# The conv's two values from the preceding half in the second state-space layer: two small VectorE operations in place of three ScalarE activations

## The chip, the cores and the metric

The kernel runs on one core of one Trainium2 chip. The metric is the device time of one execution in microseconds (us). A core has a matrix engine (TensorE, PE in the profile), a vector engine (VectorE, DVE), an activation engine (ScalarE, ACT), a general engine (GpSimd, POOL) and a queue engine that issues transfers (SyncE, SP). They run side by side, each works off its own queue in order, and they wait for each other by semaphores. SBUF is the on-chip memory of 128 partitions; PSUM is the smaller memory that TensorE writes to.

## The reference, cut to what matters

The network has four residual layers over x of shape [8, 384, 32, 32]: a state-space layer (L0), a deformable convolution (L1), a second state-space layer with a layer norm and a small MLP (L2), and a depthwise convolution with shifts (L3). The change touches L2. Its beginning, for each of the 8 samples with 1024 tokens:

```python
t = (t - mu) * jax.lax.rsqrt(var + 1e-05) * ln_w + ln_b
xz = t @ in_proj_w.T
xm, z = jnp.split(xz, 2, axis=-1)
K = conv_w.shape[-1]                      # 3
xp = jnp.pad(xm, ((0, 0), (K - 1, 0), (0, 0)))
xc = sum((xp[:, k:k + L, :] * conv_w[:, k] for k in range(K))) + conv_b
xc = jax.nn.silu(xc)
...
def step(hst, inp):
    dA_t, dBu_t, C_t = inp
    hst = dA_t * hst + dBu_t
    return (hst, jnp.einsum('bdn,bn->bd', hst, C_t))
```

Here `xm` has 768 channels. The conv runs over time, each channel by itself: a token's value is made of its own input (weight 2), the one before it (weight 1) and the one before that (weight 0). So when the 1024 tokens are worked on in two halves, the first two tokens of the second half need the last two inputs of the first half.

## The kernel before, in words

Both state-space layers are built by one function, `ssm_layer`. The change is in its inner functions `conv_last` and `conv`. A sample's 1024 tokens are cut into two halves of TS = 512 (`s["h"]` is 0 or 1), so a layer has 16 steps, one for each half. The 768 channels are cut into ND = 6 blocks of 128 partitions.

A step has 48 units: 6 channel blocks times 8 units. For each unit i, the main loop gives out the same work:

- ScalarE writes the decays `da` of unit i+2 (line 531, two instructions, into one of two PSUM tiles).
- VectorE runs the recurrence over time (`scan`, line 551, reads `da` in PSUM and `db` in SBUF).
- The states are multiplied by C: by VectorE for 5 units of 8 (line 564, `hs <- da, bc`, `da` in PSUM), by GpSimd for units 0, 2 and 5 of each block (line 562, both in SBUF; in those units the scan writes `hs` itself).
- GpSimd makes the inputs `db` of unit i+3 (line 539, `dub` times `bc`, both in SBUF). `db` has three buffers, so the `db` of unit i+3 takes the place of that of unit i, and can begin when scan i has ended.
- In the first half of a sample, ScalarE copies the last states of a unit (`keep_last`, line 557). In units 0, 2 and 5 GpSimd's line 562 overwrites `hs` in place, and so waits for that copy.
- TensorE sums over the states (line 574).

Around these, four lists written out by hand (`act`, `dve`, `pool`, `pe`, built by `plan`) say at which unit other work is put: the gate and the close of this half, the output projection and MLP of the half before, and the norm, input projection, conv and steps of the *next* half. The order of each engine's queue is as written (a manual schedule): in a unit ScalarE first takes its list, then the state copy and the decays; VectorE takes scan, product, then its list; GpSimd `db`, the product in its units, then its list.

The input projection of block d of the next half (`inner`, line 364) is put at unit 16, 17, 18, 24, 25 or 26 on TensorE. It takes one of three PSUM tiles that all projections share. One unit later ScalarE runs `conv_last`: line 389 writes bias plus the weight-2 product from PSUM to `u` in SBUF. Then:

- If the half in work is a first half, ScalarE saves the last two inputs to `halo` (line 391), a small SBUF tile of two columns for each block, for the second half of that sample.
- If it is a second half, ScalarE adds the three products of `halo` to the first two columns of `u` (line 397, three activations of one column each, `u <- halo * weight + u`).

Another unit later VectorE runs `conv` (line 405): two instructions that add the weight-1 and the weight-0 product from PSUM to `u`, over 511 and 510 columns. Behind them in VectorE's queue is the next unit's scan. In units 18 and 26 the close of a block (lines 593 and 594) stands ahead of the conv, in units 20 and 28 line 464.

The layer L0 uses `conv_last` and `conv` for its very first half alone, which is a first half; its other convs run on TensorE. So line 397 runs in L2 only: 8 second halves times 6 blocks times 3, 144 times.

Of the kernel before, what the change touches and what calls it, by code (L numbers as in the profile page):

```python
# [9 lines left out]
AF = mybir.ActivationFunctionType  # L10
ALU = mybir.AluOpType
# [73 lines left out]
V_CW, V_CB, V_DB, V_D, V_A = 0, 18, 24, 30, 36  # L85
# [17 lines left out]
class Net:  # L103
# [112 lines left out]
    def ssm_layer(self, li, src, dst, shift=None):  # L216
        tc, nc, ins = self.tc, self.nc, self.ins
# [4 lines left out]
        with ExitStack() as ctx:  # L222
# [49 lines left out]
            def v(i):  # L272
                return vec[:, i : i + 1]
# [113 lines left out]
            def conv_last(s, d):  # L387
                ps, ud = s["in", d], s["u"][:, d, :]
                nc.scalar.activation(ud, ps, AF.Identity, bias=v(V_CB + d), scale=v(V_CW + 3 * d + 2))
                if s["h"] == 0:  # L390
                    nc.scalar.copy(s["sib"]["halo"][:, d, :], ps[:, TS - 2 : TS])
                else:

                    halo = s["halo"][:, d, :]
                    for i, k, wi in ((0, 0, 0), (0, 1, 1), (1, 1, 0)):
                        c = ud[:, i : i + 1]
                        nc.scalar.activation(
                            c, halo[:, k : k + 1], AF.Identity, bias=c, scale=v(V_CW + 3 * d + wi)
                        )

            def conv(s, d):
                ps, ud = s["in", d], s["u"][:, d, :]
                w0, w1 = v(V_CW + 3 * d), v(V_CW + 3 * d + 1)
                for i, wi in ((1, w1), (2, w0)):
                    nc.vector.scalar_tensor_tensor(
                        ud[:, i:], ps[:, : TS - i], wi, ud[:, i:], ALU.mult, ALU.add
                    )
# [285 lines left out]
            def plan(prev, s, nxt):  # L693
# [54 lines left out]
                for d, t in enumerate(TI):  # L748
                    put(pe, t - 2, fetch_in, nxt, d)
                    put(pe, t, inner, nxt, d)  # L750
                    if mlp:
                        put(act, t + 1, conv_last, nxt, d)
                        put(dve, t + 2, conv, nxt, d)
                    else:
                        put(act, t + 1, conv_in, nxt, d)
                        put(pe, TCV[d], conv_pe, nxt, d)
                        put(act, TCO[d], conv_out, nxt, d)
# [35 lines left out]
            with tc.manual_schedule(engines=ENGINES):  # L793
                s = steps[0]
# [12 lines left out]
                for d in range(ND):  # L807
                    fetch_in(s, d)
                    inner(s, d)
                    conv_last(s, d)  # L810
                    conv(s, d)
                    if d == ND - 2:
                        silu(s, 0, ND // 2)
# [20 lines left out]
                for i, (s, j, m) in enumerate(units):  # L834
                    c, t = divmod(i, T)
# [1322 lines left out]
```

## Time and profile before

| what | value |
|---|---|
| median of 3 runs | 8728.45 us (8723.46 to 8728.67) |
| profiled execution, its own time | 8722.48 us |
| its span in the profile | 8720.7 us |
| granted TensorE clock, mean | 0.912 |
| GpSimd line 539, `db` | 1536 times, 2357 ns each |
| GpSimd line 562, `hs` | 576 times, 2356 ns each |
| VectorE line 551, scan into `da` | 960 times, 2285 ns each |
| VectorE line 564, product | 960 times, 1225 ns each |
| VectorE line 405, conv | 102 times 743 and 102 times 749 ns |
| ScalarE line 389, conv's first product | 102 times, median 777 ns |
| ScalarE line 391, saving `halo` | 54 times, median 149 ns |

The span is the stretch from the first to the last instruction that the profiler recorded. The profile has several views. The page gives busy times for the whole span; the groups give one line for each source line, engine and shape, with count, total busy time and mean duration (after the bar: total us, mean ns, then the idle time of the engine just before). The timeline gives instructions in order: start in us, duration in us, engine, line, operation, what is written and read, shape, and, in brackets, how long the engine sat idle before and what ended that. "x2" merges neighbours. The chain of waits is the path that ended last, followed back from the last instruction by the semaphores' times.

### The profile page before, as it was taken

Reading aid. Unit: us, or ns where it says so; the run is one execution under the profiler, and the core shown is the slowest. Engines: PE = TensorE matmul, PEld = TensorE weight load, DVE = VectorE, ACT = ScalarE, POOL = GpSimd, SP = SyncE. Lnnn points to the kernel's source line nnn. Section 1 sums busy time; section 2 is a strip of 40 time slices with the busy share of each in tenths; the row PEclk is TensorE's granted clock in tenths of the full one; section 3 lists DMA queues with packets and bytes.
Section 4 is the critical chain, followed back from the end, with each engine's and each line's share of the span. In section 5 each row is a group of like instructions: output and inputs, shape, how many; then the busy total and the mean of one; then the engine's idle time right before and its main releaser. Section 6 shows DMA issues by size and latency. Waiting matters only on the chain. (4 is left out here: it accounts for less than half of the span.)

```text
span 8720.7 us, 91254 instructions
## 1 busy us (share of the span) xinstructions
PE 7387.2 (85%) x29688; PEld 3825.2 (44%) x29688; DVE 7519.7 (86%) x8480; ACT 5832.6 (67%) x9518; POOL 5569.8 (64%) x3383
## 2 busy tenths in 40 slices
PE   7888888888886899999999985788888888888878
PEld 2232233223222788888787871233333333333323
DVE  6999999999997788988988895888988989888884
ACT  6777777777774556666666665676767777776761
POOL 6999999999998000000000005998998989898984
PEclk8899899889987999999999997898998899999989
DMA  4555555555553754565456434565666666565657
GB/s 126 126 126 123 120 124 125 118 122 125 125 126 99 186 133 110 130 166 127 103 148 159 122 76 122 131 153 144 156 156 156 149 147 153 141 157 142 154 152 152
DMA packets 796928, 1179.29 MB, mean 135 GB/s; under 512 B 260402, under 2 KB 413010, under 8 KB 762648
## 3 DMA queue, kind: packets, MB, share of 16 engines
q1 hardware_dynamic: 739444, 1157.23, 54.0%
q10 hardware_dynamic: 55540, 10.05, 0.7%
q0 software_dynamic: 1456, 6.07, 0.2%
q8 instruction: 237, 3.88, 0.2%
q14 instruction: 251, 2.06, 0.1%
HBM read 984.15 MB, written 188.98 MB: 135 GB/s over the span
## 5 line engine op out<-in xcount | busy, mean ns | idle before, releaser
L539 POOL TENSOR_TENSOR db<-dub,bc 128x1024 f32<-128x1024 f32 x1536 | 3606.2, 2357 | 369.1 <-DVE hs L551 169.1
L531 ACT ACTIVATE da<-dtb,vec 128x512 f32<-128x512 f32 x3072 | 2122.2, 691 | 610.5 <-DVE hs L564 407.9
L551 DVE TENSOR_TENSOR_SCAN da<-da,db 128x1024 f32<-128x1024 f32 x960 | 2193.2, 2285 | 130.5 <-ACT da L531 86.1
L472 POOL TENSOR_TENSOR dt<-dt,sp_e 128x512 f32<-128x512 f32 x96 | 122.3, 1274 | 2468.0 <-DMA bc<-bcd 2463.7
L1803 PE MATMUL wacc<-fsm,fxk 128*128 128x195 f32 (+21 forms) x10624 | 1574.9, 306 | 98.6 <-DVE fsm L1766 69.4
L1803 PEld LDWEIGHTS wacc<-fsm,fxk 128*128 128x128 f32 x10624 | 1481.2, 195 | 232.8 <-DVE fsm L1766 140.5
L551 DVE TENSOR_TENSOR_SCAN hs<-da,db 128x1024 f32<-128x1024 f32 x576 | 1315.3, 2283 | 195.6 <-POOL db L524 84.0
L562 POOL TENSOR_TENSOR hs<-hs,bc 128x1024 f32<-128x1024 f32 x576 | 1357.0, 2356 | 34.1 <-ACT st L557 34.1
L564 DVE TENSOR_TENSOR hs<-da,bc 128x1024 f32<-128x1024 f32 x960 | 1175.6, 1225 | 122.4 <-PE y L574 72.9
L574 PE MATMUL y<-hs,cols 128*32 128x512 f32 x6144 | 968.6, 649 | 282.5 <-POOL hs L562 260.1
L1766 DVE TENSOR_TENSOR fsm<-fhy,fhx 128x585 f32<-128x585 f32 (+39 forms) x3136 | 1011.2, 389 | 85.8 <-PE wacc L1803 77.0
L1749 DVE TENSOR_TENSOR fxk<-fxt,fwk 128x1024 f32<-128x1024 f32 (+1 forms) x688 | 813.4, 1182 | 9.7 <-DMA fxt<-fxd 8.7
L1726 ACT ACTIVATE fhy<-fpyx,cell 128x416 f32<-128x416 f32 (+10 forms) x832 | 422.4, 580 | 315.2 <-DVE fsm L1766 315.2
L574 PEld LDWEIGHTS y<-hs,cols 128*32 128x32 f32 x6144 | 189.1, 113 | 1002.4 <-issue 507.7
L651 PE MATMUL ps_m<-hid,wm 128*128 128x512 f32 x1152 | 549.9, 632 | 61.9 <-ACT hid L646 27.8
L632 PE MATMUL ps_h<-t,wm 128*128 128x512 f32 x1152 | 533.4, 607 | 56.5 <-DVE sp_e L464 24.2
L1709 ACT ACTIVATE fhx<-fpyx,cell 128x352 f32<-128x352 f32 (+9 forms) x640 | 344.5, 610 | 294.6 <-DVE fsm L1766 264.1
L364 PE MATMUL ps_in<-xn,winr 128*128 128x512 f32 x576 | 326.4, 713 | 176.6 <-ACT xn L353 127.0
L651 PEld LDWEIGHTS ps_m<-hid,wm 128*128 128x128 f32 x1152 | 226.8, 203 | 395.1 <-issue 283.5
L632 PEld LDWEIGHTS ps_h<-t,wm 128*128 128x128 f32 x1152 | 217.0, 194 | 376.6 <-issue 275.6
L583 PE MATMUL ps_z<-xn,winr 128*128 128x512 f32 x576 | 301.5, 672 | 47.7 <-DVE sp_e L464 47.7
L606 PE MATMUL ps_o<-u,wm 128*128 128x512 f32 x576 | 279.9, 636 | 41.5 <-DMA wm<-in_wout 36.3
(239 smaller groups left out, 9885.4 us busy)
## 6 DMA issues: line engine op xcount, KB each, us to landing
dtb<-dtd SPq DMA_DIRECT2D x768, 256.0 KB
dub<-dtd SPq DMA_DIRECT2D x768, 256.0 KB
fpyx<-fposd SPq DMA_DIRECT2D x104, 1024.0 KB
fxt<-fxd SPq DMA_DIRECT2D x96, 1024.0 KB
wm<-in_w SPq DMA_DIRECT2D x96, 768.0 KB
bc<-bcd SPq DMA_DIRECT2D x256, 256.0 KB
x<-x SPq DMA_DIRECT2D x73, 768.0 KB
dtd<-dt SPq DMA_DIRECT2D x192, 256.0 KB
```

The costliest lines, as they stand in the source:

```text
L531: nc.scalar.activation(da[:, i, :], s["dtb", j][:, k, :], AF.Exp, scale=na[:, j, n + i : n + i + 1])
L539: nc.gpsimd.tensor_tensor(db, du, s["bc"][p][:, 0], ALU.mult)
L551: nc.vector.tensor_tensor_scan(h1, da1, db1, 0.0, ALU.mult, ALU.add)
L562: nc.gpsimd.tensor_tensor(s["hs", m], s["hs", m], c, ALU.mult)
L564: nc.vector.tensor_tensor(hs_tile(s, m), s["da", m], c, ALU.mult)
L574: nc.tensor.matmul(s["y"][k * IP : (k + 1) * IP, :], sel, s["hs", p * NSUB + k][:, i, :], start=mlp and p == 0 and i == 0, stop=p == NQP - ...
L632: nc.tensor.matmul(ps, s["w1", q][:, k, f * P : (f + 1) * P], s["t"][:, k, :], start=(k == 0), stop=(k == G - 1))
L651: nc.tensor.matmul(ps, s["w2", q][:, f, o * P : (o + 1) * P], s["hid", q][:, f, :], start=(f == 0), stop=(f == 3))
L1726: nc.scalar.activation(hy[:, at : at + (yb - ya) * W], s["pyx", j][:, 0, ya * W : yb * W], AF.Abs, bias=bias)
L1749: nc.vector.tensor_tensor(t[:, :n], x, wk[:, j : j + 1, :].to_broadcast([P, n, P]), ALU.mult)
L1766: nc.vector.tensor_tensor(self.sub(sm, at, [(r * w, n), (w, r), (1, w)]), self.sub(hy, hy_at[by] + xa, [(r * W, n), (W, r), (1, w)]), self ...
L1803: nc.tensor.matmul(a[:, ya - 4 * o : yb - 4 * o, xa:xb], k, self.sub(sm, sm_at[by], [(w, yb - ya), (1, w)]), start=o not in s["open"], sto ...
```

## The change

For a second half, `conv_last` no longer adds the `halo` products on ScalarE. `conv` adds them on VectorE, ahead of its two large instructions: one `scalar_tensor_tensor` over two columns (`u[0:2] += w0 * halo[0:2]`) and one over one column (`u[0] += w1 * halo[1]`). Both read `halo` and `u` in SBUF and take the weight from a column of `vec` in SBUF. The sums are the same three products.

```diff
                 if s["h"] == 0:
                     nc.scalar.copy(s["sib"]["halo"][:, d, :], ps[:, TS - 2 : TS])
-                else:
-
-                    halo = s["halo"][:, d, :]
-                    for i, k, wi in ((0, 0, 0), (0, 1, 1), (1, 1, 0)):
-                        c = ud[:, i : i + 1]
-                        nc.scalar.activation(
-                            c, halo[:, k : k + 1], AF.Identity, bias=c, scale=v(V_CW + 3 * d + wi)
-                        )
 
             def conv(s, d):
                 ps, ud = s["in", d], s["u"][:, d, :]
                 w0, w1 = v(V_CW + 3 * d), v(V_CW + 3 * d + 1)
+                if s["h"] == 1:
+                    for n, k, w in ((2, 0, w0), (1, 1, w1)):
+                        nc.vector.scalar_tensor_tensor(
+                            ud[:, :n], s["halo"][:, d, k : k + n], w, ud[:, :n], ALU.mult, ALU.add
+                        )
                 for i, wi in ((1, w1), (2, w0)):
```

In the program's order 144 ScalarE instructions go and 96 VectorE instructions come, in 48 pairs. The order of all else, on every engine and queue, stays. The added lines are line 398 of the changed kernel, and the conv's large instructions become line 402.

## The prediction

> **What bounds the kernel now.** I read the busy shares, then the groups with shapes kept apart, then VectorE and GpSimd instruction by instruction around the changed place. The edit acts only in the second state-space layer (about 5300 to 8400 us), in the steps whose *next* half is a second half: 8 steps, 6 blocks each, 48 places.
>
> ```profile
> PE 7387.2 (85%) x29688; PEld 3825.2 (44%) x29688; DVE 7519.7 (86%) x8480; ACT 5832.6 (67%) x9518; POOL 5569.8 (64%) x3383
> ...
> L397 ACT ACTIVATE u<-halo,u,vec 128x1 f32<-128x1 f32 x144 | 50.5, 382 | 3.2
> ```
>
> The first line is an average over stages with different limits. In the layer that matters (stretches of 400 us between 5900 and 7100) VectorE works 354 us, GpSimd 365, TensorE 338, ScalarE 291. The second line is all that the change removes: 144 ScalarE instructions of one column, 50.5 us in total, on the engine with most room.
>
> Now VectorE around the six places of one step. Line 405 is the conv; "x2" is its two instructions.
>
> ```profile
> 6182.48 0.69 DVE L594 TENSOR_TENSOR u<-y,sz 128x512 f32<-128x512 f32 x1
> 6183.09 1.52 DVE L405 SCALAR_TENSOR_TENSOR u<-ps_in,vec,u 128x511 f32<-128x511 f32 x2
> 6184.53 2.29 DVE L551 TENSOR_TENSOR_SCAN da<-da,db 128x1024 f32<-128x1024 f32 x1
> 6186.85 1.22 DVE L564 TENSOR_TENSOR hs<-da,bc 128x1024 f32<-128x1024 f32 x1
> 6187.99 1.52 DVE L405 SCALAR_TENSOR_TENSOR u<-ps_in,vec,u 128x511 f32<-128x511 f32 x2
> 6189.44 2.29 DVE L551 TENSOR_TENSOR_SCAN da<-da,db 128x1024 f32<-128x1024 f32 x1
> ...
> 6217.41 1.52 DVE L405 SCALAR_TENSOR_TENSOR u<-ps_in,vec,u 128x511 f32<-128x511 f32 x2
> 6218.85 2.29 DVE L551 TENSOR_TENSOR_SCAN da<-da,db 128x1024 f32<-128x1024 f32 x1
> ```
>
> No line has a bracket: VectorE waits for nothing here. Each instruction starts at the end of the one before, or 0.08 us ahead of it (6183.09 + 1.52 = 6184.61, the scan starts at 6184.53). The same holds for all six places (6183.09, 6187.99, 6193.49, 6217.41, 6222.32, 6227.81). VectorE's next idle times are 1.94 us before the scan at 6213.83 and 2.40 us before the scan at 6243.11. Both end with ScalarE's `da`, and ScalarE itself had waited, idle 2.39 us at 6205.55 and 0.92 us at 6235.02, for VectorE's line 564. So a delay of VectorE in these places moves everything behind it, one for one, and the idle times don't soak it up.
>
> The chain of waits seems to say otherwise at the fourth place:
>
> ```profile
> 6217.78 0.40 ACT u L397
> 6218.20 0.67 ACT u L397 x2
> 6218.87 2.28 DVE da L551
> ```
>
> It puts the removed instructions on the path. But the scan started at 6218.85 while the conv before it ran to 6218.93; it waited for nobody, and its `da` was written by 6217.05. The chain took the last semaphore that happened to change. All chain pieces of line 397 together are 9.57 us; I count them as no gain, and keep 9.57 as the bound of a gain.
>
> **The change, part by part.** *Removed:* 3 activations at 48 places, 1.08 us of ScalarE each time (6214.47 to 6215.55). The conv starts 1.4 to 3.5 us after they end, so they cost the path nothing, and removing them brings nothing. If that cover were gone it would be worth at most 50.5 us. One thing does move: GpSimd's line 562 at 6186.46 waits for ScalarE's copy of the state (below), which is queued behind the removed instructions; it starts about 1.1 us earlier.
>
> *Added:* 48 times two VectorE instructions, 128x2 and 128x1, ahead of the conv in the same queue; no other instruction moves on any engine, and no DMA. In the program's order the first takes over the conv's wait for ScalarE, the second waits for the first, and the conv's first instruction waits for none. The nearest unhindered row is line 1427 (below): 128x1 with a per-partition pointer as here, 214 ns. A dependent instruction starts 0.03 us after the one before (1.52 less 0.741 and 0.749), an independent one 0.08 us before its end. So one place adds 0.214 + 0.03 + 0.214 - 0.08 = 0.38 us, and 48 places 18 us, if nothing hinders them. That is the lower bound of the added cost, everything on the path.
>
> *What can hinder them.* The new instructions read two tensors that both lie in SBUF (`halo` and `u`). In this layer's steps no VectorE instruction of before does: scan, product, gate, conv and residual all have one tensor in PSUM. And GpSimd is at work almost without pause:
>
> ```profile
> 6180.44 4.68 POOL L539 TENSOR_TENSOR db<-dub,bc 128x1024 f32<-128x1024 f32 x2
> 6186.46 2.36 POOL L562 TENSOR_TENSOR hs<-hs,bc 128x1024 f32<-128x1024 f32 x1 [1.34 <-ACT st L557]
> 6188.77 2.35 POOL L539 TENSOR_TENSOR db<-dub,bc 128x1024 f32<-128x1024 f32 x1
> 6191.80 2.37 POOL L539 TENSOR_TENSOR db<-dub,bc 128x1024 f32<-128x1024 f32 x1 [0.68 <-DVE da L551]
> ...
> 6215.14 4.66 POOL L539 TENSOR_TENSOR db<-dub,bc 128x1024 f32<-128x1024 f32 x2
> 6219.75 2.35 POOL L562 TENSOR_TENSOR hs<-hs,bc 128x1024 f32<-128x1024 f32 x1
> ```
>
> The trace has one place where a small VectorE instruction with two SBUF tensors meets a busy GpSimd, in another layer:
>
> ```profile
> 2823.36 8.97 POOL L1226 TENSOR_TENSOR firw<-firw 128x1078 f32<-128x1078 f32 x4
> ...
> 2827.27 5.09 DVE L1107 TENSOR_TENSOR fobk<-fobk,fob 128x1 f32<-128x1 f32 x1 [12.80 <-DMA fobk<-in_c_cols]
> ...
> L1427 DVE TENSOR_SCALAR far<-far,fob x32: 212/214/216, 2813.7 to 4922.0; 128x1 f32<-128x1 f32 x32
> ```
>
> One column takes 5.09 us, after its wait was over, and ends at 2832.36, 0.03 us after GpSimd's row of four (2823.36 + 8.97 = 2832.33). Its twin at 2809.53 took 0.52 and ended at 2810.05, as GpSimd's instruction did. Line 1427, with one SBUF tensor, keeps 214 ns whatever GpSimd does. I read it so: such an instruction waits until GpSimd pauses.
>
> I walk one step by that reading, from the rows above. GpSimd is limited too: `db` has three buffers, so the `db` of unit i+3 waits for scan i, and once VectorE is held, GpSimd soon runs dry and lets it go. Behind a held instruction the second is free, and a place costs the wait + 0.03 + 0.03 + 0.214 - 0.08 = wait + 0.19.
> - First place: asked at 6183.09, GpSimd's pair ends at 6185.12: 2.03, adds 2.22.
> - Second: GpSimd's next `db` starts when the scan ends and takes 2.36; the product covers 1.17: 1.26 remain, adds 1.45.
> - Third: the product and line 464 cover 1.76: 0.67, adds 0.86.
> - Fourth: two `db` and one `hs` in a row are ready; asked at 6217.41, free at 6222.10: 4.69, adds 4.88.
> - Fifth and sixth: as second and third, 1.45 and 0.86.
>
> Sum 11.7 us a step, 94 us in 8 steps. Lower end of the blocked case: if VectorE gets in between two GpSimd instructions of a row, the fourth place pays 0.07 for the first and 2.3 for the second, together about 2.35: 9.2 a step, 74 us. Upper end: at the first place `hs`, now 1.1 us earlier, starts at about 6185.3, just when the second small instruction wants in, and holds it for 2.3 more: 14.0 a step, 112 us. I take 94, by the row of 5.09 us, which did not get in at two joints of GpSimd's row.
>
> Held behind the blocked instruction in VectorE's queue are the conv, the next scan and product. For them wait ScalarE (two `da` buffers), GpSimd (three `db`), and TensorE (three PSUM tiles, one freed by the conv). Nothing else is late first.
>
> The Trainium skill, "SBUF — State Buffer", section "SBUF: two separate sides", says that GpSimd and a VectorE instruction with two SBUF inputs share a port pair as an exclusive lock, for whole instructions and to whoever starts first; it doesn't say who wins between two GpSimd instructions. By it alone a release at each joint would be allowed, an estimate near the 74; the row says longer. Its "Perfetto Trace Analysis", section "Optimizing Scalar/DVE Operations", puts the access overhead at about 60 ns on VectorE against 93 on ScalarE, by which 96 instructions would be an estimated 6 us and the change nearly free; the row of 214 ns and the 5.09 us speak against that. The same section advises to take work off a saturated VectorE, and this change adds to it.
>
> **The rivals.**
> - *No blocking:* only the 214 ns count, 18 us: 8722.5 + 18 = 8741. For it: no row here has this operation with a pointer and two columns. Against: 5.09 us for a column. Chance 0.14.
> - *ScalarE was on the path:* faster. The removed instructions stand in the chain at places four and five of some steps; if these entries were real, and the new instructions fell into VectorE's idle times, 9.6 us go: 8713. It decides only where `da` ends after VectorE is free; at the fourth place `da` is 1.8 us early. Chance 0.05.
> - *Blocked, but let in at each joint:* 74 us, 8796; the other end 112 us, 8834. With the forecast these hold 0.81.
>
> **How the numbers follow.** The sum stands on the profiled execution, 8722.5 us; the median is 8728.45, 0.07% above, less than the spread of the steps' walk. 8722.5 + 94 = 8816.5. That a held step passes on its delay whole is argued above; if a third were lost, the lower blocked case gives 8772, and one more catch of 1.7 us a step on top of 14.0 gives 8722.5 + 8 x 15.7 = 8848: my range. It leaves out no blocking and faster, 0.19 together. A measurement of this kernel tells about 0.2%, 17.5 us, from no change; the 18 us lie on that bound, so half of 0.14 is "same". Faster 0.05, same 0.07, slower 0.88.
>
> **What would show it.** In the profile after, line 398: mean of the first small instruction about 2 us, not 0.2, ends that fall on GpSimd's ends; the second near 0.2. The conv's own 0.74 unchanged, ScalarE 50 us less busy, the other steps as long as before. A mean near 0.2 makes me wrong by 75 us; a long line 398 with a small difference in time means that delays are soaked up after all.

## The result

| | median | runs | against before |
|---|---|---|---|
| before | 8727.11 us | 4 | |
| changed | 8805.49 us | 4 (8802.74 to 8816.66) | 1.0093 [1.0075, 1.011] |
| changed, measured again (experiment `e0_after_again`) | 8814.3 us | 4 | 1.0104 [1.0088, 1.0121] |

The second measurement stands beside 7 runs of before with a median of 8723.4 us. The change costs 0.75 to 1.2%, some 78 us in the first set of runs and 91 us in the second. Its profiled execution took 8816.66 us, 94.2 us more than the profiled execution of before.

The head of the page and the groups of the changed kernel:

```profile
PE 7418.5 (84%) x29688; PEld 3841.3 (44%) x29688; DVE 7616.6 (86%) x8576; ACT 5782.5 (66%) x9374; POOL 5569.8 (63%) x3383
...
L398 DVE SCALAR_TENSOR_TENSOR u<-halo,vec,u 128x2 f32<-128x2 f32 x48 | 64.2, 1338 | 0.0
L398 DVE SCALAR_TENSOR_TENSOR u<-halo,vec,u 128x1 f32<-128x1 f32 x48 | 37.2, 774 | 1.7
```

ScalarE lost the 50 us it was to lose. VectorE's busy time rose by 97 us (7519.7 to 7616.6), and line 398 alone has 101: 96 instructions of one or two columns, 0.77 and 1.34 us each on average. Nothing in the view says that they waited; a VectorE instruction that is held after it has started counts as busy. That gives itself away only by a duration that doesn't fit the shape.

VectorE of the changed kernel at three places of one step, the first, fourth and fifth ("x2" is the pair of line 398):

```profile
6208.87 2.29 DVE L398 SCALAR_TENSOR_TENSOR u<-halo,vec,u 128x2 f32<-128x2 f32 x2
6211.07 1.52 DVE L402 SCALAR_TENSOR_TENSOR u<-ps_in,vec,u 128x511 f32<-128x511 f32 x2
...
6247.69 4.70 DVE L398 SCALAR_TENSOR_TENSOR u<-halo,vec,u 128x2 f32<-128x2 f32 x2
6252.31 1.52 DVE L402 SCALAR_TENSOR_TENSOR u<-ps_in,vec,u 128x511 f32<-128x511 f32 x2
6253.75 2.29 DVE L548 TENSOR_TENSOR_SCAN da<-da,db 128x1024 f32<-128x1024 f32 x1
6256.07 1.23 DVE L561 TENSOR_TENSOR hs<-da,bc 128x1024 f32<-128x1024 f32 x1
6257.21 1.52 DVE L398 SCALAR_TENSOR_TENSOR u<-halo,vec,u 128x2 f32<-128x2 f32 x2
6258.65 1.53 DVE L402 SCALAR_TENSOR_TENSOR u<-ps_in,vec,u 128x511 f32<-128x511 f32 x2
```

GpSimd of the changed kernel beside the fourth and fifth place:

```profile
6245.43 4.64 POOL L536 TENSOR_TENSOR db<-dub,bc 128x1024 f32<-128x1024 f32 x2
6250.04 2.34 POOL L559 TENSOR_TENSOR hs<-hs,bc 128x1024 f32<-128x1024 f32 x1
6256.12 2.34 POOL L536 TENSOR_TENSOR db<-dub,bc 128x1024 f32<-128x1024 f32 x1 [3.74 <-DVE da L548]
```

The pair at 6247.69 ends at 6252.39, GpSimd's `hs` at 6252.38. Between the two small instructions lies 6250.09, where GpSimd's `db` ended (6250.07). The next pair begins at 6257.21, when GpSimd has been at a new `db` since 6256.12; the first of it ends at 6258.48, GpSimd at 6258.46. Ends of the small instructions that were held fall on ends of GpSimd's, 0.02 us later, all through the layer. GpSimd's mean durations stay what they were (2356 ns for `db` and for `hs`): it holds, VectorE waits.

### The profile page after: what moved, and what is told of

Read it like the earlier page. It is cut to its first block, busy times and chain, and to the rows that moved or that the text cites. A ratio compares the mean times of both kernels' runs of the same rounds, so it can differ in the third digit from the quotient of the medians.

```text
span 8814.9 us, 91206 instructions
## 1 busy us (share of the span) xinstructions
PE 7418.5 (84%) x29688; PEld 3841.3 (44%) x29688; DVE 7616.6 (86%) x8576; ACT 5782.5 (66%) x9374; POOL 5569.8 (63%) x3383
## 5 line engine op out<-in xcount | busy, mean ns | idle before, releaser
L536 POOL TENSOR_TENSOR db<-dub,bc 128x1024 f32<-128x1024 f32 x1536 | 3605.9, 2356 | 473.7 <-DVE hs L548 177.5
L559 POOL TENSOR_TENSOR hs<-hs,bc 128x1024 f32<-128x1024 f32 x576 | 1356.8, 2356 | 26.3 <-ACT st L554 26.2
L554 ACT COPY st<-da 128x2 f32<-128x2 f32 x480 | 75.8, 158 | 384.9 <-DVE hs L561 383.2
```

Source lines behind the costliest of these rows:

```text
L536: nc.gpsimd.tensor_tensor(db, du, s["bc"][p][:, 0], ALU.mult)
L559: nc.gpsimd.tensor_tensor(s["hs", m], s["hs", m], c, ALU.mult)
```

## The experiments

### e1: one operand in PSUM

```diff
-                            ud[:, :n], s["halo"][:, d, k : k + n], w, ud[:, :n], ALU.mult, ALU.add
+                            ud[:, :n], ps[:, k : k + n], w, ud[:, :n], ALU.mult, ALU.add
```

> The two small VectorE instructions stay, with the same shapes, pointer and waits, but read their first operand from the block's PSUM tile instead of halo, so one of two tensors lies in PSUM. The products of the preceding half are left out of the sum (wrong columns are added in their place). Theory (VectorE waits for GpSimd because both tensors lie in SBUF): each small instruction takes 0.2 us, a place adds 0.38 us, 48 places 18 us: about 8745 where before is 8727. Rival (two small dependent instructions on VectorE are dear in themselves, 1.3 and 0.8 us as the profile of the changed kernel has them): no change from the changed kernel, 8800 to 8815.

Measured 8747.89 us, 1.0025 [1.0016, 1.0034], 23 us over the 8724.43 us of the before measured with it (e2, e3 and e6 have the same). Line 398 of this kernel, with least, median and greatest duration in ns:

```profile
L398 DVE SCALAR_TENSOR_TENSOR u<-ps_in,vec,u x96: 207/217/220, 5400.0 to 8234.8; 128x2 f32<-128x2 f32 x48, 128x1 f32<-128x1 f32 x48
```

Same engine, same number, same shapes: 0.22 us each and never longer. From scan to scan, the six places of a step are each 0.38 us longer than before, 2.28 us a step, in the steps after the first. The steps themselves grew by 3.1 to 3.4 us; in them TensorE's long row of `ps_m` matmuls took 13.2 to 13.3 us instead of 12.56 (last section). With that, two more small instructions at each place cost 23 us; the other 55 to 68 us of the change come from where the operand lies.

### e2: behind the conv's large instructions

```diff
+                for i, wi in ((1, w1), (2, w0)):
+                    nc.vector.scalar_tensor_tensor(
+                        ud[:, i:], ps[:, : TS - i], wi, ud[:, i:], ALU.mult, ALU.add
+                    )
                 if s["h"] == 1:
...
-                for i, wi in ((1, w1), (2, w0)):
-                    nc.vector.scalar_tensor_tensor(
-                        ud[:, i:], ps[:, : TS - i], wi, ud[:, i:], ALU.mult, ALU.add
-                    )
```

> The two small instructions stand behind the conv's two large ones instead of ahead of them. Theory: the large ones cover 1.5 us of GpSimd's instruction. Walk of one step: first place waits 0.5 and adds 0.8; second, third, fifth and sixth find GpSimd idle and add 0.5 each; fourth waits 0.8, then the second small one waits for a whole GpSimd product, 3.2. Sum 5.9 us a step, 48 us in 8 steps: about 8775. Rival (price of the instructions themselves): as the changed kernel, 8800 to 8815. Rival (no gain from the order, GpSimd always in the way): the same.

Measured 8778.49 us, 1.0063 [1.005, 1.0077], 54 us over before. The fourth place, VectorE and GpSimd:

```profile
6234.35 1.52 DVE L397 SCALAR_TENSOR_TENSOR u<-ps_in,vec,u 128x511 f32<-128x511 f32 x2
6235.79 3.24 DVE L402 SCALAR_TENSOR_TENSOR u<-halo,vec,u 128x2 f32<-128x2 f32 x2
...
6232.05 4.66 POOL L536 TENSOR_TENSOR db<-dub,bc 128x1024 f32<-128x1024 f32 x2
6236.67 2.34 POOL L559 TENSOR_TENSOR hs<-hs,bc 128x1024 f32<-128x1024 f32 x1
```

The two of its pair take 0.94 us, until the end of GpSimd's `db`, and 2.27, until the end of the `hs` behind it, and the place adds 3.17 us. The first place adds 0.8, as the walk had it, in six of the eight steps (2.6 and 3.1 in the others, where the second instruction was held too). The second, third, fifth and sixth add 0.38 to 0.39 in the steps after the first, as if unhindered; the walk had 0.5. So the places of a step add 5.5 us, but most steps grew by 6.8: a scan further on waits 3.72 us for ScalarE's `da` where it waited 2.40 before. The walk left that out. Even so, the same instructions in the same number cost a third less for standing 1.5 us later.

### e3: no edges at all

```diff
-                if s["h"] == 1:
-                    for n, k, w in ((2, 0, w0), (1, 1, w1)):
-                        nc.vector.scalar_tensor_tensor(
-                            ud[:, :n], s["halo"][:, d, k : k + n], w, ud[:, :n], ALU.mult, ALU.add
-                        )
```

> Neither the three ScalarE activations nor the two VectorE instructions: the first two columns of a second half lack the products of the preceding half. Theory: the removed ScalarE work was hidden, so the time is that of before within 0.1% (8727, 8718 to 8736). Rival (ScalarE was on the path at places four and five): 10 us or more faster than before, 8717 or less.

Measured 8724.89 us against 8724.43, 1.0 [0.9991, 1.0009]. The 50 us of ScalarE work that the change took away were worth nothing in the total. The entries of line 397 in the chain of waits were not real, as the scan's missing idle time had said. At one of the 48 places ScalarE was late all the same: at the sixth place of the first step the conv of before sat idle for 2.99 us and started 0.03 us after line 397. There this kernel is 1.8 us shorter, and later waits of the same half take that back.

### e4: the ScalarE work put back beside the new

```diff
+                else:
+                    halo = s["halo"][:, d, :]
+                    for i, k, wi in ((0, 0, 0), (0, 1, 1), (1, 1, 0)):
...
```

> The changed kernel with the three ScalarE activations put back beside the VectorE instructions, so that the products of the preceding half are added twice. Theory: ScalarE's activations are hidden and cost nothing; they delay the state copy, and so GpSimd's product at the first place, by 1.1 us, so that the second small instruction there is never caught: 9.9 to 10.1 us in each of the steps, 80 us over before, about 8805, and no step with 13.6. Rival (the ScalarE work removed by the change gave something back, up to 10 us): 8813 to 8816 or more, slower than the changed kernel.

Measured 8817.0 us, 1.0106 [1.0089, 1.0123], 94 us over the 8723.4 of the before measured with it (e0, e7 and e8 have the same): what the rival forecast, not the theory. But the rival's reason isn't what the trace shows. The second small instruction of the first place took 0.22 us in every step but the first, as the theory had it: with the copy 1.1 us later the race was not lost in any of them. The places' prices are those of the changed kernel without a lost race (2.2 to 2.6, 1.44, 0.85, 4.3 to 4.7, 1.44, 0.86). The excess lies elsewhere: four steps grew by 13.1 to 13.5 us, though their places add 11.5 to 11.7. In these the long row of `ps_m` matmuls on TensorE (line 651 of before) takes 0.8 to 1.0 us more than before, in two others 0.6 less. Its granted clock differs (last section). Against the changed kernel measured in the same set of runs, 8814.3, e4 is not distinguishable (the intervals overlap almost whole).

### e6: the same sums with one operand in PSUM

```diff
                 if s["h"] == 0:
-                    nc.scalar.copy(s["sib"]["halo"][:, d, :], ps[:, TS - 2 : TS])
+                    e, last = s["sib"]["halo"][:, d, :], ps[:, TS - 1 : TS]
+                    nc.scalar.activation(
+                        e, ps[:, TS - 2 : TS], AF.Identity, bias=v(V_CB + d), scale=v(V_CW + 3 * d)
+                    )
+                    nc.scalar.activation(
+                        e[:, 0:1], last, AF.Identity, bias=e[:, 0:1], scale=v(V_CW + 3 * d + 1)
+                    )
...
                 if s["h"] == 1:
-                    for n, k, w in ((2, 0, w0), (1, 1, w1)):
-                        nc.vector.scalar_tensor_tensor(
-                            ud[:, :n], s["halo"][:, d, k : k + n], w, ud[:, :n], ALU.mult, ALU.add
-                        )
+                    nc.vector.scalar_tensor_tensor(
+                        ud[:, :2], ps[:, :2], v(V_CW + 3 * d + 2), s["halo"][:, d, :], ALU.mult, ALU.add
+                    )
```

> The same sums in another way: in the first half ScalarE writes bias and the products of the last two inputs (from PSUM) to halo, two activations in place of the copy; in the second half one VectorE instruction over two columns writes PSUM times weight 2 plus halo, ahead of the conv. One tensor in PSUM, one in SBUF. Theory: no waiting for GpSimd, one instruction of 0.21 us and a gap of 0.03 on the path at 48 places: 12 us over before, about 8739; ScalarE's extra 0.4 us a place is hidden. Rival (any small instruction here is dear, 1.3 us): 62 us over before, 8790.

Measured 8730.12 us, 1.0007 [0.9998, 1.0016]: 6 us over before, not told from no change.

```profile
L403 DVE SCALAR_TENSOR_TENSOR u<-ps_in,vec,halo x48: 207/210/219, 5401.9 to 8218.7; 128x2 f32<-128x2 f32 x48
```

This instruction reads `halo` as the changed kernel's do, and is never held. A place costs 0.25 us, 1.5 us a step, as forecast. That most steps grew by less, 0.1 us, goes with TensorE's clock again: the row of line 651 took 12.26 us instead of 12.56. If the edge has to be on VectorE, this is the way, about 80 us cheaper than the changed kernel. Of all versions none is faster than before.

### e0, e7, e8: what exactly is waited for

> The changed kernel once more, unaltered. Its profile had 13.6 to 13.8 us more in three of the eight steps and 10.1 in others: in those three the second small instruction of the first place waited 2.3 us for GpSimd's product, in the others it came just ahead of it. Theory: this is a race within 0.2 us, so the number of such steps varies from run to run, and the total lies between 80 (none caught) and 107 us (all caught) over before: 8805 to 8832. Rival (those steps are something else, say a clock): the second small instruction of the first place is 0.2 us in steps that are nevertheless 13.6 us longer.

Measured 8814.3 us, 91 over before. The number of caught second instructions is five of eight in both profiles, but they cost differently. In the first profile of the changed kernel three steps paid for both instructions (some 4.6 us at the first place); in this one only the first step did. In the other four the first instruction had been let in at a joint (the end of one GpSimd instruction with the next ready behind it) after 0.21 to 0.33 us, and the place added 2.4 to 2.6 us, little more than in the steps without a catch. So the race is real and goes by tenths of a microsecond; but it alone doesn't make the time vary from run to run, since the profile with fewer paid catches is the longer one (8818.97 against 8816.66). Three of these four steps still grew by 13.2 to 13.4 us where their places add 11.4 to 11.6; in them TensorE's long row took 13.3 to 13.6 us, 12.56 in before. For these the rival is right: it is the clock. The theory is half right.

In e7 the small instructions become plain additions, and the weights are left out:

```diff
-                        nc.vector.scalar_tensor_tensor(
-                            ud[:, :n], s["halo"][:, d, k : k + n], w, ud[:, :n], ALU.mult, ALU.add
-                        )
+                        nc.vector.tensor_tensor(ud[:, :n], s["halo"][:, d, k : k + n], ud[:, :n], ALU.add)
```

> The two small instructions as plain tensor_tensor adds of halo to u, without the pointer (the weights are left out of these products). The row of before that blocked for 5.09 us was such a plain one, and it passed two joints of GpSimd's row without getting in, while in the changed kernel each small instruction gets in at the next joint. Theory A (any small instruction with two SBUF tensors gets in at the next joint that it has waited for by 0.1 us or more): the same waits as the changed kernel, at the fourth place 2.4 and 2.3 us, 8800 to 8815. Theory B (the form decides): at the fourth place the first waits 4.7 us, through three GpSimd instructions, and the second takes 0.2; the total is the same. Rival (the pointer scalar is what makes it wait): 0.2 us each, about 8742.

Measured 8808.12 us, 1.0097 [1.008, 1.0114], theory A: 2.39 and 2.26 us at the fourth place in six of the eight steps (in one of the others the first got in at a joint 0.07 us after it asked). For the wait, form and pointer don't matter. The plain form is 0.06 us shorter where nothing holds it (0.16 against 0.22).

In e8 four `db` of a step are made by two GpSimd instructions of half the length:

```diff
+                if mlp and s["h"] == 0 and j in (2, 3) and m in (6, 7):
+                    for i in range(2):
+                        nc.gpsimd.tensor_tensor(
+                            db[:, i, :], s["dub", j][:, k, :], s["bc"][p][:, 0, i, :], ALU.mult
+                        )
+                    return
                 du = s["dub", j][:, k, :].unsqueeze(1).to_broadcast([P, 2, TS])
```

> The changed kernel with GpSimd's db of four units in a step (those that run beside the second, third, fifth and sixth place) cut into two instructions of 512 columns instead of one of 1024. Theory (the wait is for GpSimd's instruction in progress, one small instruction gets in at a joint): at the second and fifth place the first small instruction waits 0.2 instead of 1.27 us, and the second 1.2 instead of 0.22; at the third and sixth the first still waits, 0.8. The sum and the time stay within 5 us of the changed kernel: 8800 to 8820. Rival (the wait is for something else that lasts 1.3 us, VectorE's own pipeline or ScalarE): 1.27 and 0.22 as before the cut.

Measured 8814.19 us, 1.0107 [1.009, 1.0124], as long as the changed kernel. GpSimd and VectorE at the second place of one step:

```profile
7028.79 2.49 POOL L537 TENSOR_TENSOR db<-dub,bc 128x512 f32<-128x512 f32 x2 [1.35 <-DVE da L554]
...
7029.89 1.41 DVE L398 SCALAR_TENSOR_TENSOR u<-halo,vec,u 128x2 f32<-128x2 f32 x2
```

The pair still ends with GpSimd (7031.30 and 7031.28). But its two parts have changed places: the first takes 0.21 us, since GpSimd's first half ends while it asks, and the second 1.16, the other half. In the changed kernel they were 1.27 and 0.22. At the third place the first waits 0.82. VectorE waits for the GpSimd instruction in progress, and gets one small instruction in at each joint, if it asked early enough. In the profiles of the changed kernel, e0, e2, e4 and e8, of the instructions that came less than 0.4 us before a joint all 30 that came 0.13 us or less before it missed it and waited for the whole next one, and all 23 that came 0.15 us or more before it got in.

## Why the prediction was right, point by point

- *VectorE's path at the six places:* right. One step of the profile has 2.21, 1.44, 0.85, 4.62, 1.44 and 0.85 us more, 11.4 in all, against 11.7 in the walk, and the step grew by 10.4; the 1 us between goes with TensorE's clock (last section). Idle time soaked up part of the delay at one place alone, the sixth of the first step, where the conv of before had waited 2.99 us: it became 2.33 us shorter.
- *ScalarE's work hidden, gain nothing:* right in the total, shown by e3. That the conv starts 1.4 us or more after line 397 was wrong at the same one place (0.03 us).
- *Unhindered price 18 us:* e1 has 0.38 us a place as worked out, 17 us at all the places, and 23 in time. The Trainium skill's 60 ns an instruction ("Perfetto Trace Analysis", section "Optimizing Scalar/DVE Operations"), an estimated 6 us, is too little here (0.22 us each where nothing holds them); the same passage calls the 60 ns busy time and puts the profiled latency at about twice that, which the prediction left out.
- *Blocking by GpSimd where both tensors lie in SBUF:* right. e1 and e6 take the cause away, e2 the moment, e8 changes what is waited for. The rule of the skill's "SBUF — State Buffer", section "SBUF: two separate sides", agrees with the trace (one column takes 2.26 us beside GpSimd's `hs` of 2.35, and 0.22 unhindered) in all but what it leaves open, the joints.
- *The fourth place:* the sum was right (4.88 against 4.61), the step was not. The prediction let the first instruction wait through three GpSimd instructions, by the row of 5.09 us, and the second go free. In the trace the first takes 2.40 and the second 2.26: each gets in at one joint. So the forecast's sign, a mean of about 2 us for the first small instruction and near 0.2 for the second, did not come (1.34 and 0.77), though the sum of both did. The lower case was wrong there too: it let the first in at a joint that came 0.07 us after it asked, and it missed that one. That the total agrees here is partly luck: in both accounts the last release is the end of the same `hs`. e7 shows that the form is not what made the row of 5.09 us pass two joints. Why that row did is open; its GpSimd neighbours were others, and no run here repeats them.
- *The upper end, `hs` catching the second instruction of the first place:* in the profile it was paid in full in three of the eight steps, so it is part of the result and not a bound. One such step, and behind it GpSimd's `hs` at the first place of the step shown above, where it waited 0.24 us for ScalarE's state copy and the second instruction went free:

```profile
5799.26 4.68 DVE L398 SCALAR_TENSOR_TENSOR u<-halo,vec,u 128x2 f32<-128x2 f32 x2
...
5796.96 4.67 POOL L536 TENSOR_TENSOR db<-dub,bc 128x1024 f32<-128x1024 f32 x2
5801.57 2.35 POOL L559 TENSOR_TENSOR hs<-hs,bc 128x1024 f32<-128x1024 f32 x1
...
6211.12 2.35 POOL L559 TENSOR_TENSOR hs<-hs,bc 128x1024 f32<-128x1024 f32 x1 [0.24 <-ACT st L554]
```

- *8816.5 us:* the profiled execution took 8816.66, the medians 8805.5 and 8814.3. Part of that closeness is chance. The places of the eight steps add 96.0 us where the walk had 94: three lost races bring 6 more, the first step 3 less, the other four 1 less. TensorE's clock, which the walk left out, comes on top, and the two medians, 9 us apart for one kernel, show how far the time moves.

## What to carry to other kernels

Before moving a tiny instruction to VectorE, look where its tensors lie and what GpSimd does at that moment: two tensors in SBUF beside a busy GpSimd cost the rest of GpSimd's instruction, here up to 2.4 us for one or two columns, and the profile shows it as busy time. One operand in PSUM, or a place just after GpSimd has run dry, takes the wait away. And work on an engine that is ahead can be worth nothing, here 144 instructions of it; a chain of waits that names it is checked by the idle time of the instruction it is said to hold.

## What was not expected of the hardware

TensorE's granted clock in one and the same piece of work depended on when it came. The columns are the stretch and its length, busy us and instruction count of PE, PEld, DVE, ACT and POOL, then the granted clock, the share of the DMA engines and GB/s. Each pair of rows is the same row of 24 matmuls of line 651 (648 in the changed kernel, 655 in e4), which TensorE works through without a pause, cut where the clock changes; the counts take in neighbours at the edges. Before, 12.56 us:

```profile
6253.73:6257.77 4.04, 4.04 (x6) 1.85 (x6) 4.01 (x3) 3.75 (x7) 4.04 (x3) 0.50 1.05 284
6257.77:6266.29 8.52, 8.52 (x21) 3.77 (x20) 7.37 (x7) 3.76 (x8) 7.15 (x4) 1.00 0.47 108
```

The changed kernel, 11.98 us, in a step of 10.4 us more (11.4 at its places):

```profile
6290.92:6293.79 2.87, 2.87 (x5) 1.32 (x5) 2.87 (x2) 2.62 (x6) 2.87 (x3) 0.50 1.05 287
6293.79:6302.90 9.11, 9.11 (x23) 4.09 (x22) 8.49 (x8) 4.89 (x9) 8.30 (x4) 1.00 0.58 135
```

e4, 13.55 us, in a step of 13.4 us more (11.6 at its places):

```profile
6699.25:6705.29 6.04, 6.04 (x8) 2.52 (x8) 5.12 (x4) 5.32 (x10) 6.04 (x4) 0.50 0.99 262
6705.29:6712.80 7.51, 7.51 (x19) 3.39 (x18) 6.25 (x5) 2.19 (x5) 5.14 (x3) 1.00 0.31 65
```

The clock recorded here is full or half, nothing between. Counted at half its length, the stretch at 0.50 gives the same work each time: 4.04/2 + 8.52, 2.87/2 + 9.11 and 6.04/2 + 7.51 are all 10.5 us. So the row takes longer by half of what the half-speed stretch covers of it, 4.04, 2.87 or 6.04 us. In before the row took 12.55 or 12.56 us in six steps one after the other; in most of the longer steps the stretch falls elsewhere. What sets it off, no row here shows, and no run changed the clock alone.

Against the sum of its places a step of these versions came out between 1.5 us shorter (e6) and 2.0 us longer (e0). Not all of that was traced to TensorE's rows, but it fits e4, 13 us above its walk, and e6, 6 us below. Differences below some 10 us between versions of this kernel are of that size, and not to be read as a price of the edit.
